# Attention scores as 32-row products in four quarters of the array instead of 64-row products in two halves

## The chip, the cores and the metric

The kernel runs on one core of one Trainium2 chip. The metric is the device time of one execution in microseconds (us). It is given as the median of three runs. A profile comes from one further execution that a hardware profiler recorded. The engines are called by the names of that profile: PE is TensorE (PEld its weight loads), ACT is ScalarE, DVE is VectorE, POOL is GpSimd, SP is SyncE, whose queue issues most DMAs. PSUM is the accumulator memory that PE writes, 8 banks of 128 partitions by 512 fp32 values.

## The reference

The model is a chain of four layers on an image of 48 channels and 128x128 pixels. The change is in the first, a single-head attention over all N = 16384 pixels.

```python
qkv = jnp.einsum('bchw,oc->bohw', x, qkv_w)              # 48 -> 144 channels
qkv = conv3x3_depthwise(qkv, dw_w)
q, k, v = ...                                            # each (b, 16384, 48)
q, k = _l2norm(q), _l2norm(k)
attn = softmax(jnp.einsum('bnc,bmc->bnm', q, k) * temperature, axis=-1)
out = jnp.einsum('bnm,bmc->bnc', attn, v)
return jnp.einsum('bchw,oc->bohw', out, proj_w)
```

The later layers (sweeps of 1-D convolutions, a patch layer and a state-space scan) are not touched.

## The kernel before

**First stage (`attention`, L156).** The image is normalised and convolved on PE, eight image rows (1024 pixels) at a time (`conv`, `take`). `take` leaves the normalised queries and keys of these pixels in fp32. `split` (L410) rounds each to a high part of reduced fp32 ("fp32r") on ACT and takes the remaining low part on POOL. Queries go to a DRAM tensor `qm`, from which `moving(c)` (L196) later fetches chunk `c` of 512 queries. Keys stay in on-chip memory as `kh` (high) and `kl` (low); `join` (L211) copies the first 32 rows of both into further tiles, which the products read as `x`. Early in this stage, between the arrival of the image and the group statistics, `forms` (L120) issues 52 products of zeros on PE: full products of 128 rows, and sets of four products of 32 rows or two of 64 rows, each in its own part of the array.

**Attention proper (`attend`, L481).** There are 32 chunks of 512 queries and 128 tiles of 128 keys. The array is split into two halves of 64 rows. Partitions 0 to 63 hold the first half of the pixels as keys and partitions 64 to 127 the second, so that the two halves of the array compute two key tiles at the same time. A score tile (128 keys by 512 queries) needs 48 channels times three combinations of parts (high with high, high with low, low with high), which are packed into three products of 64 rows: these are `s<-m,kh`, `s<-m,kl` and `s<-m,x` in the profile. Each score tile takes one PSUM bank, from a pool of seven (`ps_s`, L497); the eighth bank is `acc` (`ps_a`).

Six pairs of tiles make a group (`G = 6`, L492), so a chunk has ten groups of twelve tiles and one of eight. `group` (L517) issues a group's scores on PE and the exponentials on ACT (`e<-s,temp`). In the first two pairs of a group DVE copies the second tile out of its bank whole (`e<-s` on DVE), and ACT takes its exponential later from the copy (`e<-e,temp`), in a group of six pairs. `sums` (L539) adds `e` times the values `v` into `acc`: these are full-fp32 products of 128 rows and 64 columns, two at a time in the two halves of the columns, and each is two instructions in the trace (`acc<-e,v`). PE runs the scores of one group, then the sums of the group before it, then the scores of the next.

The order on PE, ACT and DVE is as written: the wrapper `InOrder` (L39) chains each engine's instructions in the order of the calls. Once per chunk `Finish` copies `acc` out (`both<-acc`, on ACT), divides by the softmax's denominator on DVE and writes the result. Another function, `attend_shifted`, is for large temperatures; it is compiled too, but a branch on the temperature skips it here.

Of the kernel before, what the change touches and what calls it, by code (L numbers as in the profile page):

```python
# [19 lines left out]
F32 = mybir.dt.float32  # L20
# [7 lines left out]
C = 48  # L28
H = W = 128
N = H * W  # L30
# [89 lines left out]
def forms(pe, psum, pool):  # L120


    zero = pool.tile([128, CH], F32R, name="rn")
    pe.tc.nc.gpsimd.memset(zero.bitcast(F32), 0.0)
    out = [psum.tile([128, CH], F32, name="p") for _ in range(4)]

    def one(o, at, to, n):
        w, x = zero[at, n : n + to.stop - to.start], zero[at]
        pe.matmul(o[to], lhsT=w, rhs=x, start=True, stop=True)

    def pieces(size):
        return [slice(i, i + size) for i in range(0, 128, size)]

    def full(n):
        for i in range(n):
            one(out[i % 4], slice(0, 128), slice(0, 128), 0)

    def quads(n):
        for _ in range(n):
            for o, at in zip(out, pieces(32)):  # L140
                one(o, at, slice(0, 128), 0)

    full(4)
    quads(5)
    full(4)
    quads(1)
    full(4)
    quads(1)
    full(4)
    for _ in range(4):  # L150
        for o, at in zip(out, pieces(64)):
            one(o, at, slice(0, 128), 0)


@with_exitstack
def attention(ctx, tc, x1, mp, const, ins):  # L156
# [20 lines left out]
    qm = dram.tile([64 + C, N], F32, name="qm")  # L177
    kv = ctx.enter_context(tc.tile_pool(name="l0_kv", bufs=1))

    kh, kl = (kv.tile([128, HALF], F32R, name=n) for n in ("kh", "kl"))  # L180
    rest_k = []

# [12 lines left out]

    def moving(c):  # L196

        m = mp.tile([128, 2, CH], F32R, name="m")
        high, low = qm[0:C, c * CH : (c + 1) * CH], qm[C:, c * CH : (c + 1) * CH]
        for half in range(2):  # L200
            at = 64 * half
            for i, to, x in (
                (0, 0, high),
                (0, C, low[C:]),
                (1, 0, low[0:32]),
                (1, 32, low[0:32]),
            ):
                nc.sync.dma_start(m[at + to : at + to + x.shape[0], i].bitcast(F32), x)
        return m

    def join(cols):  # L211

        i = cols.start // PART
        if len(rest_k) == i:
            rest_k.append(images.tile([128, PART], F32R, name=f"x{i}"))
        to = slice(cols.start - i * PART, cols.stop - i * PART)
        for half in range(2):
            at = 64 * half
            for n, t in enumerate((kh, kl)):
                nc.sync.dma_start(  # L220
                    rest_k[i][at + 32 * n : at + 32 * n + 32, to].bitcast(F32),
                    t[at : at + 32, cols].bitcast(F32),
                )
# [5 lines left out]
    with ExitStack() as a:  # L229
# [3 lines left out]
        fp = a.enter_context(tc.tile_pool(name="l0_f", bufs=4))  # L233
        once = a.enter_context(tc.tile_pool(name="l0_a1", bufs=1))
# [15 lines left out]
        wt = wp.tile([128, 4, 256], F32, name="wt")  # L250
        nc.vector.tensor_mul(wt[:, :, 64:], raw[1], raw[0])
        nc.vector.tensor_copy(wt[:, :, 0:64], wt[:, :, 128:192])
# [14 lines left out]
        values = wt[:, :, 192:256]  # L267
# [11 lines left out]
        forms(pe, ps, rnp)  # L279
# [53 lines left out]
        def conv(p, pv, te, y, first):  # L333

            t, e = te
            both = slice(64, 192) if first >= HALF else slice(0, 128)
# [23 lines left out]
            for dx in range(3):  # L360
                for n in range(2):
                    pe.matmul(
                        rows(half[n]),
                        lhsT=wt[:, dx, 192:256],
                        rhs=t[:, y + 4 * n : y + 4 * n + 4, dx : dx + W],
                        start=(dx == 0),
                        stop=False,
                    )
            for n in range(2):
                rest(half[n], n, slice(192, 256))  # L370

        def take(t0, p, pv):
# [23 lines left out]
            kb = 64 * (t0 // HALF)  # L396
            tk = t0 % HALF
            tv = slice(t0 // 128, t0 // 128 + 8)

            qb = 64 - kb  # L400
# [9 lines left out]
            def split(act, get):  # L410

                for n in range(2):
                    f, hl = own[n], get("hl", n)
                    fq, fk = f[qb : qb + 64], f[kb : kb + 64]
                    hq, lq = hl[qb : qb + 64], hl[kb : kb + 64]
                    at = slice(tk + n * CH, tk + (n + 1) * CH)
                    to = slice(t0 + n * CH, t0 + (n + 1) * CH)
                    act.copy(hq.bitcast(F32R), fq)
                    act.copy(kh[kb : kb + 64, at], fk)
                    nc.gpsimd.tensor_sub(lq.bitcast(F32R), fq, hq)  # L420
                    nc.gpsimd.tensor_sub(
                        kl[kb : kb + 64, at], fk, kh[kb : kb + 64, at].bitcast(F32)
                    )
                    nc.sync.dma_start(qm[0:C, to], hq[0:C])
                    nc.sync.dma_start(qm[C : 64 + C, to], lq)
                if kb:
                    join(slice(tk, tk + 2 * CH))

            def get(name, n):
                return fp.tile([128, CH], F32, name=name)  # L430
# [9 lines left out]
        for b in range(NB):  # L440
# [3 lines left out]
            for y in range(0, R, 8):  # L444
# [3 lines left out]
                conv(p, pv, cur, y, t0)  # L448
# [10 lines left out]
    keys = kh, kl, rest_k  # L459
    with tc.If(small <= bits) as near:  # L460
        attend(tc, keys, v, moving, first, x1, temp, const, ins, last[0:2])
# [19 lines left out]
def attend(ctx, tc, keys, v, moving, m, x1, temp, const, ins, last):  # L481
# [9 lines left out]
    KT = N // 2 // 128  # L491
    G = 6  # L492

    ep = ctx.enter_context(tc.tile_pool(name="l0_e", bufs=G + 4))
# [4 lines left out]


    sides = [slice(0, 64), slice(64, 128)]

    def scores(m, j):
        s = [ps_s.tile([128, CH], F32, name="s") for _ in sides]
        for n in range(3):
            k, at = key_tile(keys, n, j)
            for half, part in enumerate(sides):
                pe.matmul(
                    s[half],
                    lhsT=k[part, at],  # L510
                    rhs=m[part, n // 2],
                    start=(n == 0),
                    stop=(n == 2),
                )
        return s, ep.tile([128, 2, CH], F32, name="e")

    def group(m, js, help):  # L517

        waiting, es = [], []

        def exp(e, half, s):
            act.activation(e[:, half], s, AF.Exp, scale=temp)

        for n, j in enumerate(js):
            s, e = scores(m, j)
            if help and len(js) > 4 and n < 2:
                exp(e, 0, s[0])
                dve.tensor_copy(e[:, 1], s[1])
                waiting.append(e)
            else:  # L530
                exp(e, 0, s[0])
                while waiting:
                    t = waiting.pop(0)
                    exp(t, 1, t[:, 1])
                exp(e, 1, s[1])
            es.append((j, e))
        return es

    def sums(acc, j, e):  # L539

        for half, to in enumerate(sides):
            pe.matmul(
                acc[to],
                lhsT=v[:, half * KT + j, :],
                rhs=e[:, half, :],
                start=(j == 0),
                stop=(j == KT - 1),
            )
# [5 lines left out]
    class Finish:  # L554


        def __init__(self, c, acc):
# [5 lines left out]
            act.copy(self.both, acc)  # L563
# [35 lines left out]
    names = {("f", 0): "xres", ("f", 1): "both", ("hl", 0): "second", ("hl", 1): "y"}  # L599
    own = {key: spare(name) for key, name in names.items()}  # L600

    def get(name, n):
        return own[name, n]
# [4 lines left out]
    behind, finish, acc, ahead = [], None, None, m  # L608
    for c in range(NQ):
        m = ahead  # L610
        for g in range(-(-KT // G)):
            es = group(m, range(g * G, min((g + 1) * G, KT)), c > 0 or g > 1)
            if c and g == 1:
                finish.divide()
            if c and g == 2:
                finish.result()
            if g == 0 and c + 1 < NQ:
                ahead = moving(c + 1)
            if c == 0 and g == 2:
                split(act, get)  # L620
            for i, e in behind:
                if i == 0:
                    acc = ps_a.tile([128, CH], F32, name="acc")
                sums(acc, i, e)
# [3 lines left out]
    for i, e in behind:  # L628
        sums(acc, i, e)
    end()  # L630


def key_tile(keys, n, j):

    if n < 2:
        return keys[n], slice(j * 128, (j + 1) * 128)
    per = keys[2][0].shape[1] // 128
    return keys[2][j // per], slice(j % per * 128, (j % per + 1) * 128)
# [3 lines left out]
def attend_shifted(ctx, tc, keys, v, moving, m, x1, absT, sgn, const, ins, last):  # L642
# [5 lines left out]
    KC = HALF // CH  # L648
# [10 lines left out]
    own = {name: ep.tile([128, 2, CH], F32, name="e") for name in ("f", "hl")}  # L659

    def get(name, n):
        return own[name][:, n]
# [4 lines left out]
    k16 = k16p.tile([128, HALF], F16, name="k16")  # L667
    for i in range(0, HALF, 2048):
# [1368 lines left out]
```

## Time and profile before

| what | us |
|---|---|
| median of three runs (lowest, highest) | 7174.86 (7173.81, 7175.15) |
| profiled execution, its own time | 7166.1 |
| its span, first to last instruction | 7164.0 |
| first stage, up to the first scores | 0 to 244 |
| attention proper | 253 to 3551 |
| later layers | 3551 to 7164 |

The page of the profile lists for each group of instructions its engine, the tiles it writes and reads, shapes, count, busy time and the mean duration of one. A timeline lists single instructions in order of time, with neighbours of the same kind merged: start, length of the merged stretch, count, and in brackets how long the engine had been idle and who ended that. Durations of pipelined instructions overlap, on PE and on ACT, so the distance from start to start is the rate and the duration is the latency.

### The profile page before, as it was taken

What the parts mean: (1) busy time and instruction counts of PE and PEld (TensorE: products, weight loads), DVE (VectorE), ACT (ScalarE), POOL (GpSimd) and SP (SyncE); (2) the same over time, 40 slices, a digit from 0 to 9 for tenths busy, and PEclk for the clock granted to TensorE, in tenths of its full rate; (3) what the DMA queues carried; (4) which work ended last, traced back from release to release, by engine and by line L of the source; (5) the groups of instructions that cost most, each with busy time, mean ns of one, the idle gap of its engine ahead of it and who ended that gap; (6) DMA issues with size and microseconds to landing.
All of it is one profiled execution on the core that took longest, in us unless ns stands there. A gap on an engine that the chain in (4) does not pass through costs nothing.

```text
span 7164.0 us, 200017 instructions
## 1 busy us (share of the span) xinstructions
PE 5826.9 (81%) x89756; PEld 3507.7 (49%) x89756; DVE 3844.0 (54%) x3616; ACT 4601.6 (64%) x6795; POOL 2866.4 (40%) x656
## 2 busy tenths in 40 slices
PE   9999999999999999999999998455555545554555
PEld 3455555555555555555577754343434434344444
DVE  6322212221221122112244544899999999999998
ACT  3677777777777777777741033666666666666665
POOL 3200000000000000000100322899999999999998
PEclk9999999999999999999999999677676766776667
DMA  4200000000000000000010010566566665666775
GB/s 90 54 7 10 10 8 7 10 9 7 10 10 9 7 10 10 9 7 10 17 30 12 16 46 19 156 166 161 160 159 162 162 160 154 165 165 167 179 178 149
DMA packets 201829, 515.82 MB, mean 72 GB/s; under 512 B 41859, under 2 KB 73650, under 8 KB 199058
## 3 DMA queue, kind: packets, MB, share of 16 engines
q1 hardware_dynamic: 189335, 493.23, 26.6%
q8 instruction: 705, 11.55, 0.7%
q10 hardware_dynamic: 11627, 9.71, 0.6%
q14 instruction: 162, 1.33, 0.1%
HBM read 447.73 MB, written 29.36 MB: 67 GB/s over the span
## 4 chain that ended last, share of the span: by engine, by line
PE 60%; DVE 25%; issue 6%; POOL 4%; ACT 2%; DMA 2%; SPq 0%; ACTq 0%; DVEq 0%; POOLq 0%
PE acc L49 25%; DVE h L1789 23%; PE s L49 21%; PE p L49 7%; POOL h L49 3%; PE y L49 2%; PE pp L49 1%; PE pv L49 1%; PE pc L49 1%; DMA du<-rep 1%; DVE xb L49 1%; ACT dA L49 1%; PE po L49 1%; DVE y L49 0%; ACT L49 0%
## 5 line engine op out<-in xcount | busy, mean ns | idle before, releaser
L49 ACT ACTIVATE e<-s,temp 128x512 f32<-128x512 f32 x3460 | 2141.6, 698 | 775.9 <-PE s L49 769.6
L49 POOL TENSOR_TENSOR h<-du,bt 128x3072 f32<-128x3072 f32 (+1 forms) x386 | 2560.1, 6670 | 97.1 <-DMA du<-rep 53.2
L1789 DVE TENSOR_TENSOR_SCAN h<-dA,carry,h 128x1024 f32<-128x1024 f32 x864 | 1939.5, 2324 | 31.6 <-ACT dA L49 26.8
L49 DVE COPY e<-s 128x512 f32<-128x512 f32 x636 | 440.0, 692 | 2626.9 <-PE s L49 2611.9
L49 ACT ACTIVATE dA<-dt,a 128x1024 f32<-128x1024 f32 x1152 | 1287.3, 1118 | 855.7 <-DVE h L1789 845.7
L49 PE MATMUL acc<-e,v 128*64 128x512 f32 x8192 | 1835.2, 596 | 0.0
L49 PE MATMUL y<-h,cw 128*32 128x48 f32 x49152 | 893.1, 245 | 928.6 <-issue 489.7
L49 PEld LDWEIGHTS y<-h,cw 128*32 128x32 f32 x49152 | 804.2, 139 | 1049.6 <-issue 646.8
L854 POOL MEMSET xb<- 128x256 f32 (+1 forms) x2 | 0.8, 410 | 3271.7 <-ACT absT L465 3271.7
L49 PEld LDWEIGHTS acc<-e,v 128*64 128x64 f32 x8192 | 557.0, 137 | 1093.0 <-issue 1090.2
L49 PE MATMUL s<-m,kh 64*128 64x512 f32 x4096 | 848.6, 409 | 8.1 <-ACT e L49 6.5
L49 PE MATMUL s<-m,kl 64*128 64x512 f32 x4096 | 811.8, 391 | 0.0
L49 PE MATMUL s<-m,x 64*128 64x512 f32 x4096 | 801.6, 387 | 0.0
L1789 DVE TENSOR_TENSOR_SCAN h<-dA,h 128x1024 f32<-128x1024 f32 x288 | 635.4, 2271 | 37.3 <-ACT dA L49 29.0
L49 PEld LDWEIGHTS s<-m,kh 64*128 64x128 f32 x4096 | 386.1, 184 | 371.2 <-issue 259.5
L49 PEld LDWEIGHTS s<-m,x 64*128 64x128 f32 x4096 | 387.8, 185 | 89.1
L49 ACT ACTIVATE e<-e,temp 128x512 f32<-128x512 f32 x636 | 420.7, 711 | 0.0
L49 PEld LDWEIGHTS s<-m,kl 64*128 64x128 f32 x4096 | 386.2, 184 | 69.1
L49 PE MATMUL yz<-ev,sel 128*8 128x48 f32 x4096 | 192.6, 260 | 270.6 <-ACT ev L49 268.2
L49 PEld LDWEIGHTS yz<-ev,sel 128*8 128x8 f32 x4096 | 162.2, 106 | 330.3 <-ACT ev L49 302.6
L49 PE MATMUL p<-xb,l_w 112*48 112x78 f32 (+8 forms) x6096 | 226.7, 223 | 17.6 <-DVE xb L49 6.9
L49 PE MATMUL p<-xa,l_w 112*48 112x78 f32 (+8 forms) x6096 | 228.6, 224 | 14.7 <-DVE xa L49 5.9
(223 smaller groups left out, 3915.7 us busy)
## 6 DMA issues: line engine op xcount, KB each, us to landing
du<-rep SPq DMA_DIRECT2D x768, 256.0 KB
dt<-rep SPq DMA_DIRECT2D x768, 256.0 KB
m<-qm SPq DMA_DIRECT2D x128, 64.0 KB
m<-qm SPq DMA_DIRECT2D x64, 96.0 KB
rep<-dd SPq DMA_DIRECT2D x24, 192.0 KB
yd<-ys ACTq DMA_DIRECT2D x256, 12.0 KB
qm<-hl SPq DMA_DIRECT2D x30, 128.0 KB
rest<-xa SPq DMA_DIRECT2D x90, 38.0 KB
```

The source lines that it names most:

```text
L49: ins = method(*args, **kwargs).ins
L854: nc.gpsimd.memset(b[:, lines, pad], 0.0)
L1789: nc.vector.tensor_tensor_scan(h[:, p, k, :], dA, h[:, p, k, :], carry[:, i, k : k + 1] if ci else 0.0, ALU.mult, ALU.add,)
```

## The change

Keys are laid out in one tensor `keys` of 128 partitions by 3 parts by 4096 pixels, a quarter of the pixels in each 32 partitions. Part 0 holds the high parts of channels 0 to 31, part 1 their low parts, and part 2 the high and the low parts of channels 32 to 47, 16 rows each. The queries of a chunk are laid out alike in `mq`, four times. A score tile is now five products of 32 rows (`PASSES`), and the array's four quarters of rows work on four key tiles at once. `turn(n)` issues round `n`: one product in each quarter. The quarters are out of step (`LEAD`), so that their tiles end in different rounds.

A group is eight tiles, in ten rounds, and a chunk has sixteen groups. Of the first three tiles to end in a group, DVE copies the last 224 of the 512 columns to the tile of exponentials, ACT takes the exponential of the first 288 straight from the bank, and after the group's other tiles one ACT instruction takes the exponential of the three copied pieces in place. `acc` is copied out by DVE (`Finish.take`), after the third tile of group 1. The exponentials' tiles are the four `x` tiles that held the image. `split` makes one rounding and one difference over 128 partitions where it made two over 64, and sends keys and queries on by DMA. `join` and `forms` are gone.

```diff
-def forms(pe, psum, pool):
...
-    kh, kl = (kv.tile([128, HALF], F32R, name=n) for n in ("kh", "kl"))
+    keys = kv.tile([128, 3, N // 4], F32R, name="keys")
...
+    mq = [kv.tile([128, 4, CH], F32R, name=f"mq{n}") for n in range(2)]
     def moving(c):
-        m = mp.tile([128, 2, CH], F32R, name="m")
...
+        m = mq[c % 2]
+        src = parts_of[:, :, c * CH : (c + 1) * CH]
+        for r in range(0, 128, 32):
+            nc.sync.dma_start(m[r : r + 32, 0:2].bitcast(F32), src[0:32])
+            for at in (r, r + 16):
+                nc.sync.dma_start(m[at : at + 16, 2:4].bitcast(F32), src[32:C])
         return m
-    def join(cols):
...
-        forms(pe, ps, rnp)
...
             def split(act, get):
...
-                    act.copy(hq.bitcast(F32R), fq)
-                    act.copy(kh[kb : kb + 64, at], fk)
-                    nc.gpsimd.tensor_sub(lq.bitcast(F32R), fq, hq)
...
+                    act.copy(hl[:, 0].bitcast(F32R), f)
+                    nc.gpsimd.tensor_sub(hl[:, 1].bitcast(F32R), f, hl[:, 0])
+                    nc.sync.dma_start(parts_of[:, :, to], hl[0:C])
+                    nc.sync.dma_start(keys[r : r + 32, 0:2, kc].bitcast(F32), hl[64:96])
+                    for i in range(2):
+                        nc.sync.dma_start(
+                            keys[r + 16 * i : r + 16 * i + 16, 2, kc].bitcast(F32),
+                            hl[96 : 64 + C, i],
+                        )
...
 def attend(...):
-    G = 6
-    ep = ctx.enter_context(tc.tile_pool(name="l0_e", bufs=G + 4))
+    R = 4
+    KT = N // 128 // R
+    PASSES = ((0, 0), (0, 1), (1, 0), (2, 2), (2, 3))
+    NP = len(PASSES)
+    LEAD = (0, 0, 1, 3)
+    G = 8
+    ROUNDS = G * NP // R
+    SHARED = 3
+    OWN = 288
...
     ps_s = ctx.enter_context(tc.tile_pool(name="l0_ps", bufs=7, space=PSUM))
     ps_a = ctx.enter_context(tc.tile_pool(name="l0_pa", bufs=1, space=PSUM))
...
+    def turn(n):
+        done = []
+        for r, lead in enumerate(LEAD):
+            at, i = divmod(n + lead, NP)
+            c, j = divmod(at, KT)
+            if n + lead < 0 or c == NQ:
+                continue
+            if i == 0:
+                banks[r] = ps_s.tile([128, CH], F32, name="s")
+            part, x = PASSES[i]
+            rows_ = slice(32 * r, 32 * r + 32)
+            pe.matmul(
+                banks[r],
+                lhsT=keys[rows_, part, j * 128 : (j + 1) * 128],
+                rhs=queries[c][rows_, x],
+                start=(i == 0),
+                stop=(i == NP - 1),
+            )
+            if i == NP - 1:
+                done.append((r * KT + j, banks[r]))
+        return done
...
+        for n in range(ROUNDS):
+            for j, s in turn((c * KT * NP) + g * ROUNDS + n):
...
+                if help and len(es) < SHARED:
+                    dve.tensor_copy(e[:, OWN:], s[:, OWN:])
+                    exp(e[:, :OWN], s[:, :OWN])
+                else:
+                    exp(e, s)
+                es.append((j, e))
+                if then and len(es) == SHARED:
+                    then()
+        if help:
+            late = first[:, 0:SHARED, OWN:]
+            exp(late, late)
...
-            act.copy(self.both, acc)
+            self.acc = acc
+
+        def take(self):
+            dve.tensor_copy(self.both, self.acc)
```

## Prediction

> **What bounds the kernel now.** First the busy times by stretch, to see which engine fills the attention; then the chain that ended last, for the period of a group; then single instructions in the timeline, for rates and latencies.
>
> ```profile
> 253.00:3551.00 3298.00, 3296.79 (x20461) 1682.31 (x20461) 645.14 (x826) 2516.01 (x4132) 5.13 (x4) 1.00 0.03 9
> ```
>
> The columns after the length are PE, PEld, DVE, ACT, POOL, the granted clock and DMA. PE fills the stretch at clock 1.00, ACT 76% of it. The chain between 900 and 1100 us is PE alone:
>
> ```profile
> 954.19 4.35 PE s L49 x36
> 958.54 5.30 PE acc L49 x24
> 963.84 2.99 PE s L49 x24
> ```
>
> A group is 4.35 + 5.30 = 9.65 us. The last group of a chunk has 24 score products (2.99), and its sums, 16 instructions, take 1.72 less than 24 (four steps of 0.43, below). A chunk is 11 x 9.65 - 1.36 - 1.72 = 103.07, 32 chunks 3298: the whole stretch.
>
> One group in the timeline:
>
> ```profile
> 1008.88 0.50 PE L49 MATMUL s<-m,kh 64*128 64x512 f32 x2
> 1009.22 0.40 PE L49 MATMUL s<-m,kl 64*128 64x512 f32 x2
> 1009.46 0.40 PE L49 MATMUL s<-m,x 64*128 64x512 f32 x2
> ...
> 1009.95 2.08 ACT L49 ACTIVATE e<-s,temp 128x512 f32<-128x512 f32 x3 [2.30 <-PE s L49]
> 1010.00 1.39 DVE L49 COPY e<-s 128x512 f32<-128x512 f32 x2 [8.26 <-PE s L49]
> ...
> 1012.91 0.39 PE L49 MATMUL s<-m,x 64*128 64x512 f32 x2
> 1013.15 4.15 ACT L49 ACTIVATE e<-s,temp 128x512 f32<-128x512 f32 x7
> ...
> 1013.23 5.37 PE L49 MATMUL acc<-e,v 128*64 128x512 f32 x24
> 1013.71 0.14 PEld L49 LDWEIGHTS acc<-e,v 128*64 128x64 f32 x2 [0.29 <-issue]
> ```
>
> Two half-array products go together as one round. The first step after a switch of form is 0.34 (1008.88 to 1009.22), the others 0.23. From the last scores to the first sums it is 0.32; sums step by 0.48, then 0.43 (the next weight loads start at 1014.14 and 1014.57). Of the 5.30, 0.48 + 10 x 0.43 leaves 0.52 for the switch back. A bank's last product starts at 1009.46, ACT on it at 1009.95, DVE at 1010.00: 0.49 and 0.54 until a reader starts. Seven exponentials fit in 4.15 though the page gives each 0.698: they start 0.57 apart.
>
> **Rounds of four quarters.** The change's form stands in this trace, in `forms`; the timeline of the weight loads alone, each of which goes just ahead of its product:
>
> ```profile
> 26.79 1.00 PEld L49 LDWEIGHTS p<-rn 32*128 32x128 f32 x20 [0.37 <-issue]
> 28.16 0.76 PEld L49 LDWEIGHTS p<-rn 128*128 128x128 f32 x4 [0.37 <-issue]
> 29.28 0.19 PEld L49 LDWEIGHTS p<-rn 32*128 32x128 f32 x4 [0.36 <-issue]
> 29.71 0.30 PEld L49 LDWEIGHTS p<-rn 128*128 128x128 f32 x2 [0.24 <-issue]
> ```
>
> Five rounds of four take 28.16 - 26.79 = 1.37 us, one round 0.43, switches included. A further round is (1.37 - 0.43) / 4 = 0.235, as for two halves: four products cost what two did. A group of eight tiles then has 10 rounds, the last starting at 0.34 + 8 x 0.235 = 2.22; 0.32 to the sums; 8 steps of sums and the way back, 0.48 + 6 x 0.43 + 0.52 = 3.58. That is 6.12 us, times 512 groups 3133: 165 less than 3298. Ten rounds for eight tiles in place of twelve save more than 160 more groups, with their switches, cost.
>
> The Trainium skill (TensorE: Matmul & The Clock Gate, Measured speedup vs the span model) measured four row tiles of 32 rows by 512 columns at 3.07 times one, not 4. By that a round would be 4 / 3.07 x 0.235 = 0.306, an estimate, and 5120 rounds 364 us dearer. The rows above, taken on this core, decide.
>
> **The banks.** This is the step that decides. The order of the changed program, with its waits, shows what a released bank does. Seven banks go round in the order in which tiles are begun. Counting rounds from 0: quarters 0 and 1 begin tiles in rounds 0 and 5 and end them in 4 and 9, quarter 2 begins in 4 and 9, quarter 3 in 2 and 7. Eight begin per group, and each takes the bank of the tile seven before. So quarter 1's tile in round 5 takes the bank of quarter 3's that was begun in round 7 of the group before and gets its last product in round 1 of this group. Between lie four rounds, 0.94 us. PE's instruction waits for ACT's first exponential of the group, and that for DVE's copy of the same tile: the two engines drain a bank one after the other.
>
> From the first score's start: round 1 starts at 0.34. DVE starts 0.54 later, at 0.88. Its copy of 224 columns: the page has 0.692 for 512; other DVE rows give 1.04 ns per column (0.240 for 78, 0.692 for 512), so 0.39, end 1.27. ACT follows DVE by 0.03 (in the scan, a DVE record ends at 5005.273 and ACT starts at 5005.307): 1.30. Exponential of 288 columns: 0.69 for 512 less 224 x 0.83 ns (1.118 us for 1024 against 0.698), so 0.50, end 1.80. Release to PE, from the first group of chunk 0, where PE waits for ACT:
>
> ```profile
> 258.18 0.76 ACT L49 ACTIVATE e<-s,temp 128x512 f32<-128x512 f32 x1
> ...
> 258.99 0.18 PEld L49 LDWEIGHTS s<-m,kh 64*128 64x128 f32 x1 [0.39 <-ACT e L49]
> 258.99 0.50 PE L49 MATMUL s<-m,kl 64*128 64x512 f32 x1
> 259.32 0.39 PE L49 MATMUL s<-m,kl 64*128 64x512 f32 x1
> ```
>
> 0.05 from the end of the exponential (258.94) to PE: 1.85. Round 5 was due at 0.34 + 4 x 0.235 = 1.28, so PE stands 0.57. After such a wait the next round comes 0.34 later (258.99 to 259.32), not 0.235, since the weights were not loaded ahead: 0.10 more. Behind the waiting product stand quarters 2 and 3 in the same round and all that follows, the sums too. A group becomes 6.12 + 0.67 = 6.79, and 512 make 3476, 178 more than 3298. Even is at (3298 - 3133) / 512 = 0.32 per group.
>
> Other releases, with round 5 at 1.85, round 7 at 2.43 and round 9 at 2.90: the second shared tile (ended in round 3, 0.81) is copied from 1.35, exponential from 1.77, free at 2.32 for round 7; the third (round 4) free at 2.71 for round 9. Margins 0.1 and 0.2 are less than a round, by which weights are loaded ahead, so each may cost up to 0.1. ACT: five exponentials at 0.57, three of 288 columns at 0.57 - 0.19 = 0.38, and one of 672 from on-chip memory, (1.32 - 0.71) + 0.13 = 0.74: 4.74 per group, below 6.12. It ends its late piece at about 6.2, and its next exponential is due at 6.79 + 1.30.
>
> Bounds of the stall. Below: copy 0.35; exponential 0.41 (the page's ACT copy of 288 columns); no cost of refilling. Free at 0.88 + 0.35 + 0.03 + 0.41 + 0.05 = 1.72, stall 0.44: 3358, +60. Above: both margins missed, 0.2 more: 3579, +281. I take 0.67, all of whose terms come from the nearest rows.
>
> **The rest.** `forms` gone: the statistics' aggregate ends at 30.06 and its product on PE starts at 33.54 behind `forms`, so 3.4 us gained; PE idles longer there and its clock, 0.50 from 38 to 48 us already, may take that back (0 to -3.4; I take -3). `split` on ACT and POOL halves, but PE is busy 100% between 100 and 200 us, which hides it. In its last call two POOL differences (1.26 each) go, but eight DMAs on SP's queue remain at 0.5 each, so ACT's first exponential at 252.46 stays, +-2 us. `both<-acc` on DVE (0.69) follows the third copy, about 2.1 to 2.8, before the sums at 3.2; the divide behind it on DVE (0.42 + 0.68 + 3.34) ends at 7.3, before the next group's first copy at 6.79 + 0.88 = 7.67. The queries' DMAs are issued fifteen groups ahead of their use. `attend_shifted` is not run.
>
> Sum: +178 - 3 = +175, on the profiled 7166.1: 7341. The median stands 8.8 above that execution, so I forecast 7174.86 + 175 = 7350.
>
> **Rivals.**
> 1. The drain is quicker than PE's need (faster). If both engines read one bank at once, it is free at 0.34 + 0.49 + 0.50 + 0.05 = 1.38: stall 0.10 + 0.10, 512 x 6.32 = 3236, -62, time about 7110 (with no stall at all -165 and 7007). It decides once the bank is free by 1.28 + 0.32 - 0.10 = 1.50 instead of 1.85. Against it: the changed program has ACT wait for DVE, and the bounds above stay over 0.32. For it: all four quarters need not stand still in hardware as they do in my sum. 0.11, and 0.02 for a tie.
> 2. The clock falls (slower). PE would wait once in each group, 0.6 of 6.8 us. Before, with PE waiting 0.39 for each exponential, the windows show 0.50 in 252 to 256 us, after an idle stretch, 0.93 in 256 to 260 and 1.00 in 262 to 272: short waits did not bring it down. Halving it for 5% of the stretch costs 174 more: 7524. It leaves my range once 3% of the stretch runs at half (106 of 3476). 0.05.
> 3. The four quarters don't run together while ACT and DVE read other banks, the change not doing what it says: at two by two, 5120 x 0.235 = 1203 more. No sign of it in `forms`, where nothing was read meanwhile. 0.02.
>
> The skill (same page, A second HAM failure mode: psum-queue depth-cycling) describes rival 2, short idle times at PSUM that make the clock swing. In the row above they did not; by the rule the time would be rival 2's.
>
> **How the numbers follow.** My forecast has 0.80, between 7174.86 + 60 - 3 = 7232 and 7174.86 + 281 = 7456. To leave no more than two in ten out I reach down to 7195, a stall of 0.37, toward rival 1. Slower by over 0.2% (14 us, about what can be told from no change) 0.87, within 0.02, faster 0.11.
>
> **What would show it.** PE idle before `s`, some 0.6 us once per group, ended by ACT's exponential of 288 columns; group period 6.79; rounds 0.235 apart; DVE's 224 columns 0.39 and the 288 columns 0.50 long; clock 1.00. It is wrong if the 288-column exponential starts before DVE's copy of that tile ends, if round 5 follows round 4 without a gap, or if the period is under 6.44.

## The result and the profile after

The changed kernel takes 7347.64 us (median of four runs, 7346.34 to 7354.23). The kernel before took 7175.0 us in the runs beside it, and the ratio of the runs is 1.0243, 95% interval 1.0225 to 1.0261: slower by 2.4%. The forecast was 7350.

The profiled execution took 7346.34 us, with a span of 7344.5. The attention, from the first score product to the last sum, is 3482.7 us long where it was 3305.6, so 177.1 us of the 180.5 by which the span grew lie there. The same stretch that carried the reading of before, with the columns as there (PE, PEld, DVE, ACT, POOL, granted clock, DMA):

```profile
253.00:3730.00 3477.00, 3383.12 (x28620) 1561.48 (x28616) 769.29 (x1751) 2521.03 (x4602) 2.52 (x2) 1.00 0.05 14
```

The clock is 1.00 as before, and no engine but PE is near its limit. PE is no longer busy throughout. The chain that ended last was PE alone; now it runs through three engines in this and other groups:

```profile
913.51 0.40 DVE x L49
913.91 0.02 issue
913.93 0.51 ACT x L49
914.45 0.04 issue
914.49 1.43 PE s L49 x17
915.92 3.58 PE acc L49 x16
```

DVE copies 224 columns out of a bank, 0.02 later ACT takes the exponential of the other 288, and 0.04 to 0.05 after that PE can start a product into this bank. The four pieces ahead of PE's product are 0.98 us long. The timeline of one group, PE's weight loads and the queues left out, shows where PE stood meanwhile:

```profile
1000.93 1.66 PE L49 MATMUL s<-mq,keys 32*128 32x512 f32 x21
1001.80 1.07 DVE L49 COPY x<-s 128x224 f32<-128x224 f32 x3 [5.71 <-issue]
1002.23 4.18 ACT L49 ACTIVATE x<-s,temp 128x288 f32<-128x288 f32 x8 [1.86 <-DVE x L49]
...
1002.78 1.43 PE L49 MATMUL s<-mq,keys 32*128 32x512 f32 x19 [0.19 <-ACT x L49]
...
1004.15 3.65 PE L49 MATMUL acc<-x,v 128*64 128x512 f32 x16
```

ACT's merged line is three exponentials of 288 columns and five of 512. The first 21 of a group's 40 score products go without a break: five rounds of four, and quarter 0 of round 5. The 22nd is the tile of quarter 1 that waits for its bank. It starts 1.85 after the group began (1000.93 to 1002.78), after DVE at 0.87 and ACT at 1.30. In the medians over the 354 groups between 1000 and 3400 us quarter 0 starts round 5 at 1.27 and quarter 1 at 1.846, a gap of 0.575. The next group starts at 1007.73, and the median period is 6.790.

The page's table must be read with care here:

```profile
L49 DVE COPY x<-s 128x224 f32<-128x224 f32 x1530 | 547.8, 388 | 2692.2 <-issue 2184.7
L49 PE MATMUL s<-mq,keys 32*128 32x512 f32 x20480 | 1589.0, 412 | 95.8 <-ACT x L49 94.5
```

It puts PE's idle time for ACT at 94.5 us, 0.19 for each of 511 waits, a third of the gap. A product's record lasts about 0.4 us while the next starts 0.23 later, so the records of the products before the wait reach into it. What a wait costs is read from start to start.

### The profile page after: what moved, and what is told of

The parts are those of the page before. It is cut to its first block, busy times and chain, and to the rows that moved or that the text cites. A ratio compares the mean times of both kernels' runs of the same rounds, so it can differ in the third digit from the quotient of the medians.

```text
span 7344.5 us, 215883 instructions
## 1 busy us (share of the span) xinstructions
PE 5902.6 (80%) x97896; PEld 3381.2 (46%) x97896; DVE 3968.3 (54%) x4540; ACT 4589.7 (62%) x7242; POOL 2825.8 (38%) x623
## 4 chain that ended last, share of the span: by engine, by line
ACT 29%; DVE 27%; PE 24%; issue 14%; POOL 4%; DMA 2%; SPq 1%; ACTq 0%; DVEq 0%; POOLq 0%
ACT x L49 27%; DVE h L1767 21%; PE p L49 7%; PE acc L49 6%; PE s L49 4%; DVE x L49 3%; POOL h L49 3%; PE y L49 2%; PE pp L49 1%; DMA du<-rep 1%; DVE xb L49 1%; PE pc L49 1%; ACT dA L49 1%; PE pv L49 1%; PE po L49 1%
## 5 line engine op out<-in xcount | busy, mean ns | idle before, releaser
L49 ACT ACTIVATE x<-s,temp 128x512 f32<-128x512 f32 (+1 forms) x4096 | 2145.1, 630 | 951.7 <-DVE x L49 951.7
L49 DVE COPY x<-s 128x224 f32<-128x224 f32 x1530 | 547.8, 388 | 2692.2 <-issue 2184.7
L49 PE MATMUL acc<-x,v 128*64 128x512 f32 x8192 | 1871.0, 599 | 0.0
L49 PE MATMUL s<-mq,keys 32*128 32x512 f32 x20480 | 1589.0, 412 | 95.8 <-ACT x L49 94.5
L49 PEld LDWEIGHTS s<-mq,keys 32*128 32x128 f32 x20480 | 1023.0, 183 | 853.7 <-ACT x L49 730.0
L49 PEld LDWEIGHTS acc<-x,v 128*64 128x64 f32 x8192 | 542.6, 136 | 1064.7 <-issue 1053.2
L49 ACT ACTIVATE x<-x,temp 128x672 f32<-128x672 f32 x510 | 457.6, 897 | 0.0
L49 PEld LDWEIGHTS p<-xb,l_w 112*48 112x48 f32 x6096 | 193.3, 123 | 51.6 <-DVE xb L49 36.3
L49 PEld LDWEIGHTS p<-xa,l_w 112*48 112x48 f32 x6096 | 192.6, 122 | 49.6 <-DVE xa L49 30.8
L49 PE MATMUL pc<-wt,xa 128*128 128x288 f32 x768 | 198.2, 415 | 0.0
```

Of the source, the lines that this page charges most:

```text
L49: ins = method(*args, **kwargs).ins
```

## Experiments

In the first four runs the kernel before took 7166.58 us beside them, in the last four 7167.94. Ratios are to these. The expectations start from 7347, which stood beside a kernel before of 7175.0, so some 8 us of each difference in time are the runs' and not the edit's.

**ACT drains every bank alone** (`e1_act_alone`):

```diff
-                if help and len(es) < SHARED:
-                    dve.tensor_copy(e[:, OWN:], s[:, OWN:])
-                    exp(e[:, :OWN], s[:, :OWN])
-                else:
-                    exp(e, s)
+                exp(e, s)
```
(and without the late exponential)

> ACT drains all eight tiles of a group alone; the copies by DVE and the late exponential are gone. Theory (PE waits in round 5 for the bank of the first tile drained, free at 0.34 + 0.54 + 0.39 + 0.03 + 0.50 + 0.05 = 1.85 us after the group's first score): by ACT alone the bank is free at 0.34 + 0.49 + 0.69 + 0.05 = 1.57, so the first wait shrinks by 0.28, but the third bank, behind two exponentials of 512 columns, now comes 0.1 too late for round 9 and costs 0.2 with the refill. Period 6.80 - 0.28 + 0.2 = 6.72, time about 7347 - 40 = 7307. Rival A (ACT's work sets the period, as its share of the chain suggests): its work per group falls from about 4.95 to 8 x 0.57 = 4.56, time about 7347 - 0.39 x 512 = 7147. Rival B (two engines drain faster than one): slower than 7347.

It took 7331.97 us, ratio 1.0231 (1.0214 to 1.0248), with a period of 6.769, where 7307 and 6.72 were expected. The ratio alone doesn't tell it from the changed kernel, whose interval overlaps; the trace does. ACT's work as the bound (7147) is excluded. Round 5 goes on at 1.600 instead of 1.846:

```profile
1000.41 1.23 PEld L49 LDWEIGHTS s<-mq,keys 32*128 32x128 f32 x21 [0.81 <-issue]
...
1001.29 4.73 ACT L49 ACTIVATE x<-s,temp 128x512 f32<-128x512 f32 x8 [2.06 <-PE s L49]
...
1002.03 0.99 PEld L49 LDWEIGHTS s<-mq,keys 32*128 32x128 f32 x17 [0.39 <-ACT x L49]
1003.19 0.18 PEld L49 LDWEIGHTS s<-mq,keys 32*128 32x128 f32 x2 [0.16 <-ACT x L49]
```

So the help of DVE, put in front of ACT's exponential of the same bank, makes the first bank come free 0.25 us later than ACT alone would. The period falls by 0.02 only, because the third bank now comes late. In the medians over some 440 groups ACT's second exponential ends at 2.13, so with the 0.05 of the release the second bank is free at 2.18, just when quarter 3 starts its tile in round 7 (2.18). That tile is not late, but its next product follows 0.34 later instead of 0.23. The third exponential ends at 2.71; its bank is free at 2.76 and holds up quarter 2 in round 9 (2.756 instead of 2.64; the last line above).

**The third tile copied whole by DVE, the first two by ACT alone** (`e2_third_by_dve`):

```diff
-                if help and len(es) < SHARED:
-                    dve.tensor_copy(e[:, OWN:], s[:, OWN:])
-                    exp(e[:, :OWN], s[:, :OWN])
+                if help and len(es) == SHARED - 1:
+                    dve.tensor_copy(e, s)
```
(and the late exponential over the third tile alone)

> The first two tiles of a group are drained by ACT alone; the third is copied whole by DVE and its exponential taken last. Theory: first bank free at 1.57 (wait 0.29 + 0.10), second at 1.41 + 0.69 + 0.05 = 2.15 for round 7, due at 2.15, third at 1.04 + 0.54 + 0.69 + 0.05 = 2.32 for round 9, due at 2.6: one wait of 0.39 in place of 0.67. Period 6.80 - 0.28 = 6.52, time about 7347 - 143 = 7204. Rival A (ACT's work): 8 x 0.57 + 0.04 = 4.60 per group, time about 7165, the same as with ACT alone within 20 us. Rival B (drained by two engines is faster): slower than 7347.

7271.65 us, ratio 1.0148 (1.0131 to 1.0165), period 6.641 where 7204 and 6.52 were expected. The wait for the third bank is gone and the first is as in the run above (1.59). The missing 0.11 is the second bank, free at 2.17 (the exponential ends at 2.12) and taken at that moment: the next product of that quarter comes at 2.51 instead of 2.40. Two engines on different banks are here better than two on one bank, but one drain of 1.23 us still does not fit into four rounds.

**All quarters in step** (`e3_in_step`):

```diff
-    LEAD = (0, 0, 1, 3)
+    LEAD = (0, 0, 0, 0)
```

> LEAD = (0, 0, 0, 0): the four quarters begin and end their tiles in the same rounds; the work of each engine is unchanged. Theory: in round 5 the fourth tile needs the bank of the first one ended in round 4, started at 1.04, free at 1.04 + 0.54 + 0.39 + 0.03 + 0.50 + 0.05 = 2.55, where round 5 is due at 1.28: wait 1.27 + 0.10 in place of 0.67. Period 6.80 + 0.70 = 7.50, time about 7347 + 358 = 7705. Rival A (ACT's work) and any theory in which rounds or switches of form cost more: no work changes, 7347 within 20 us.

7683.27 us, ratio 1.0725 (1.0707 to 1.0743), period 7.438, against 7705 and 7.50:

```profile
1004.82 1.67 PE L49 MATMUL s<-mq,keys 32*128 32x512 f32 x23
...
1007.32 1.43 PE L49 MATMUL s<-mq,keys 32*128 32x512 f32 x17 [0.83 <-ACT x L49]
```

All four tiles now end in round 4, and quarter 3's tile of round 5 stands until 2.498 after the group's start (2.55 expected). The offset of the quarters is worth 0.65 us per group. The loss follows the time from a tile's last product to the product that takes its bank, as the theory says.

**A short drain of the first three banks** (`e4_short_drain`). The first three tiles are read over 8 columns only, and three full exponentials from the fourth tile's bank take the place of theirs. ACT's work is not less than in the first run (eight full exponentials and three short ones); the three banks are free almost at once. The result is not the attention's any more; the run serves the timing alone.

```diff
-                if help and len(es) < SHARED:
-                    dve.tensor_copy(e[:, OWN:], s[:, OWN:])
-                    exp(e[:, :OWN], s[:, :OWN])
+                if len(es) < SHARED:
+                    exp(e[:, :8], s[:, :8])
...
+                if len(es) == SHARED + 1:
+                    for i in range(SHARED):
+                        exp(es[i][1], s)
```
(and without the late exponential)

> The first three tiles of a group are read by ACT over 8 columns only, so that their banks come free early; their exponentials are then taken from the fourth tile's bank, so three of eight tiles have another tile's exponentials. ACT still takes eight exponentials of 512 columns per group, PE does the same products, DVE drains nothing. Theory: the first bank is free at 0.34 + 0.49 + 0.27 + 0.05 = 1.15, before round 5 at 1.28: no wait, period 6.10 to 6.15, time 7347 - 0.70 x 512 = 6990 to 7015, also 160 below the kernel with two halves. Rival A (ACT's work, 8 x 0.57 + 3 x 0.15 = 5.0 per group, not less than now): 7347 or more. Rival C (rounds of four quarters, or switches of form, cost more beside the drains than in the zero products of the trace before): a fall of less than half of that, 7180 to 7347.

7007.16 us, ratio 0.9779 (0.9762 to 0.9795), period 6.122:

```profile
1001.28 2.61 PE L49 MATMUL s<-mq,keys 32*128 32x512 f32 x40
1002.07 0.27 ACT L49 ACTIVATE x<-s,temp 128x8 f32<-128x8 f32 x1 [0.55 <-PE s L49]
1002.53 5.11 ACT L49 ACTIVATE x<-s,temp 128x8 f32<-128x8 f32 x10 [0.19 <-PE s L49]
1003.81 3.65 PE L49 MATMUL acc<-x,v 128*64 128x512 f32 x16
```

All 40 products of a group go in one run, rounds 0.23 apart, and the attention takes 3141.7 us, 163.9 less than before. That is the gain of the rounds by themselves. With the changed kernel's period it makes the stall 6.790 - 6.122 = 0.668 us. It also excludes ACT as the bound: here it works more, 2744 of 3137 us (87%) against 2521 of 3477, and PE is busy 3134.5 of the 3137.

**Groups of four tiles** (`e5_groups_of_four`). If the loss is a bank that is wanted back too early, sums between its last product and its next tile should remove it, at the price of twice as many switches between scores and sums.

```diff
-    LEAD = (0, 0, 1, 3)
-    G = 8
+    LEAD = (0, 0, 0, 0)
+    G = 4
```
(and ACT alone, as in the first run)

> The changed kernel with groups of four tiles in place of eight: all quarters in step, five rounds to a group, every bank drained by ScalarE alone. A tile then takes the bank of the tile seven before it, which is the first tile of the group before or a tile of the group before that: free 1.2 us after the fifth round starts, while PE is in its sums (1.9 us). Theory (the drain of one bank against four rounds is the loss): no wait ended by ScalarE before a score product, a period of 1.04 + 0.32 + 0.48 + 2 x 0.43 + 0.52 = 3.22 us for four tiles (6.43 for eight, where the changed kernel has 6.79), 1024 x 3.22 = 3297 in place of 512 x 6.79 = 3476, so about 180 us under the changed kernel, within 0.3% of the kernel before on either side. Rival (ScalarE's own rate or something else about products of 32 rows beside a drain is what costs): PE still stands in front of scores and the period for four tiles is near 3.4, the time within 60 us of the changed kernel.

7182.63 us (7174.82 to 7191.08), ratio 1.0019 (1.001 to 1.0028). In the timeline PE's lines have no idle time in brackets, and its pieces follow one another without a gap:

```profile
1000.69 1.44 PE L49 MATMUL s<-mq,keys 32*128 32x512 f32 x20
...
1002.05 1.94 PE L49 MATMUL acc<-x,v 128*64 128x512 f32 x8
...
1003.92 1.44 PE L49 MATMUL s<-mq,keys 32*128 32x512 f32 x20
```

The period is 3.237 for four tiles, 6.47 for eight, where the kernel before needs 9.646 x 8 / 12 = 6.43. The expectation had 3.22; the rest is 0.01 each in the way to the sums (0.33) and in the sums with the way back (1.87), which over 1024 groups are 17 us. The attention takes 3317.5 us, 12 more than before: the saved rounds go into the switches.

**The kernel before without `forms`** (`e6_before_no_forms`):

```diff
-        forms(pe, ps, rnp)
```

> The kernel before, without the call of forms. The prediction took 3 us for this part of the change (0 to 3.4); the two traces showed the first convolution 2.1 us earlier. Theory: 1 to 3 us under the kernel before, the first products of the convolution at about 41.7 in place of 43.6 us, the clock at 0.50 from about 30 us on. Rival (the time comes back further on, because the idle stretch takes the clock down): no difference in the start of the attention, 252.5 us.

7162.61 us, ratio 0.9989 (0.998 to 0.9998). The first lines are of the kernel before, the second pair of this run:

```profile
43.56 7.80 PE L49 MATMUL p<-band,wt 128*128 128x512 f32 x12
...
58.34 5.32 PE L49 MATMUL p<-band,wt 128*128 128x512 f32 x12
```

```profile
41.67 7.47 PE L49 MATMUL p<-band,wt 128*128 128x512 f32 x12
...
56.13 5.32 PE L49 MATMUL p<-band,wt 128*128 128x512 f32 x12
```

The convolution starts 1.9 us earlier and is 2.2 us ahead in its second round. The first exponential of the attention keeps that lead (250.25 against 252.46). The product after the statistics' aggregate starts 3.07 us earlier (30.47 against 33.54). In between the products of `p<-band,ident` take 7.16 us instead of 6.33, and the granted clock from 30 to 50 us is 0.60 instead of 0.74: part of the gain goes to the clock. The medians differ by 5.3 us, more than the 2.2 that the traces show; the interval holds both.

**Four `hl` buffers in the first stage** (`e7_four_hl`). In the first stage the changed kernel's trace has a wait of PE that no step of the prediction names:

```profile
ACT hl L49 <- DMA keys<-hl: 21.9, 10, 7.6
```

```profile
179.04 3.68 PE L49 MATMUL pss<-sq,blk 128*128 128x512 f32 x4 [2.09 <-ACT sq L49]
```

The first is from the list of waits (us in total, times, longest), the second from the timeline. The rounding into `hl` has to wait until the DMAs have emptied the buffer, and on ACT the squares `sq` for the norms stand behind it. PE waits 2.09 us for them, and the four products then take 3.68 us. The run gives every second call of `split` two more buffers:

```diff
+                if name == "hl" and (t0 // (2 * CH)) % 2:
+                    return mq[1][:, 2 * n : 2 * n + 2].bitcast(F32)
```

> The changed kernel, in which split writes into four hl buffers in turn in place of two (the other two lie in the second buffer of the queries, which is free in that stage). Theory (the wait of ScalarE's cast for the DMA that empties hl holds up the squares queued behind it, PE stands 2.1 us at 177 us and the clock falls to 0.50 for 3.4 us): ScalarE's waits for that DMA, 21.9 us in 10, are gone or nearly so, PE is busy without a break from 100 to 200 us with the clock at 1.00, and the attention starts about 4 us earlier (245.9 to about 242); the time is 4 us or 0.05% lower, at the edge of what the comparison can tell. Rival (PE's idle time there comes from the DMA queue itself, not from the number of buffers): the same 2 us of PE idle, and the attention starts at 246.

The waits for the DMA are gone and PE does not stand:

```profile
100.00:200.00 100.00, 100.00 (x330) 37.43 (x330) 77.28 (x52) 32.20 (x58) 21.88 (x25) 1.00 0.54 116
```

```profile
177.64 1.98 PE L49 MATMUL pss<-sq,blk 128*128 128x512 f32 x4
```

The first scores, of the changed kernel and then of this run:

```profile
245.89 2.10 PE L49 MATMUL s<-mq,keys 32*128 32x512 f32 x25 [1.26 <-ACT late L49]
```

```profile
242.79 2.10 PE L49 MATMUL s<-mq,keys 32*128 32x512 f32 x25 [1.26 <-ACT late L49]
```

They start 3.1 us earlier. So the number of buffers was the cause of the wait. The size of the gain is less sure: in the five other runs with two buffers the first scores start at 244.1 to 247.4 us, with four, here and in the last run, at 242.8 and 243.3. The time, 7344.92 us, ratio 1.0244 (1.023 to 1.0258), does not show it: from the last sum on, the later layers, the same in all runs, took between 3611 and 3623 us in the profiled executions.

**Groups of four and four `hl` buffers together** (`e8_both`), the edits of the two runs.

> Groups of four tiles and four hl buffers together. Theory: the two savings add, about 184 us under the changed kernel and 4 us under the groups of four alone: 0.9985 to 0.9998 of the kernel before. Rival: the groups of four already show what there is, and nothing is added.

7177.77 us, ratio 1.0011 (1.0002 to 1.002), 4.9 under the groups of four alone; the intervals of the two overlap, so that the savings add is not shown, nor that they don't. It is slower than expected because the period is 3.235 and not 3.22. The only version under the kernel before that keeps the whole computation is that kernel without `forms`.

## Why the prediction was right

**The rounds of four quarters.** Forecast 0.235 us a round, 6.12 a group, 165 us less. Measured without the stall: 0.233, 6.122 and 163.9 less. A round of four takes as long as the round of two did before, also while ACT and DVE read other banks; rival 3 falls. The Trainium skill's page TensorE: Matmul & The Clock Gate, section Measured speedup vs the span model, has a speed-up of 3.07 for four row tiles. By that the prediction estimated a round at 0.306; the short drain's rounds took 0.233, and the measurement decides.

**The banks.** Each link was there: DVE at 0.87 after the group's start (0.88), the copy 0.39 to 0.40 long (0.39), ACT at 1.30 (1.30), its exponential 0.50 (0.50), PE at 1.85 (1.85), the stall 0.575 (0.57), the next round 0.34 later (0.34). The period of 6.79 is the forecast's. The experiments show that it is this chain: a quick drain gives the whole 0.668 back, a drain by one engine gives 0.25 back at this bank, more distance between last product and next tile gives it back too, and less distance makes it longer. The other two margins, 0.1 and 0.2, were left open at up to 0.1 each; they cost nothing in the changed kernel. They were larger than the sum had them, 0.18 and 0.25: DVE's second copy starts at 1.26 and not at 1.35, and the two banks are free at 2.24 and 2.63, for products at 2.42 and 2.88. In the second experiment, where a bank came free at the moment it was wanted, that did cost the 0.11.

**Rivals 1 and 2.** Rival 1 said that two engines might read one bank at once. The program has ACT wait for DVE, and ACT followed DVE 510 times; most of the 951.7 us that ACT stood ahead of that, 1.87 each time, it would have stood for the scores. What two readers at once would do, no run here shows. The rival's other half was that a stall below 0.32 would make the change faster. The short drain, with no stall, is faster. That its 7007.16 is the very time that the rival named is luck: it lies 159 us under the kernel before of its own runs, where the rival had 168. Rival 2: a wait of 0.575 in every 6.79 us left the clock at 1.00 in the 3477 us of the attention. The Trainium skill (TensorE: Matmul & The Clock Gate, A second HAM failure mode: psum-queue depth-cycling) tells of short idle times between products that make the clock swing; these waits did not.

**The small terms** were less good. `forms` gave 2.1 us, not 3: the clock took more back than I allowed. That `split` costs nothing because PE is busy 100% between 100 and 200 us failed. Its cover was gone since the change itself put a new wait ahead of PE's work: PE was busy 97.91 of those 100 us. The lead of 2.1 us that `forms` gave was a lag of 1.7 at the first score (245.89 against 244.17), so 3.9 us were lost between: 2.1 of PE standing, and most of the rest in the four products behind it (3.68 us instead of 1.98), at a lower clock (0.94 from 170 to 200 us). Four buffers gave 3.1 of it back, by one execution of each. I had looked at the two engines whose work was halved, and not at the DMAs that must empty the buffer before ACT may fill it again, nor at what stands behind `split` on ACT. ACT's first exponential came 3.8 us earlier (248.66), outside the 2 us allowed: before, ACT's load of the table ahead of it stood 4.52 us for the DMA `qm<-hl`, and now it does not.

By profiled executions the sum is off by 5: 180.2 us more where 175 were forecast, and the missed 3.9 is most of that. By medians it is off by 2.4 the other way. The step that took the 8.8 us between the median and the profiled execution of before over to after has no ground: after's profiled execution lies 1.3 us under its median. That the forecast of 7350 is only 2.4 off is so in part luck: the 8.8 too much covers the 5 and the 1.3 too little. A difference of some us between two executions is not the kernel's.

## What to carry to other kernels

When products become quicker, work out anew when each PSUM bank is wanted back: from the last product of a tile to the first product of the tile that takes its bank, against the whole drain, with the start of the reader and the release. Where the program has a second engine's help on the same bank come in series, it lengthens that drain, as here; give the help another bank, or put other work of PE between, which costs more switches between forms (groups of four took the stall away and were still 0.2% over the kernel before). A form with fewer rounds is worth what is left after the wait, and a run of the same kernel with the drain cut short tells at once how much that could be.

## What the runs showed of the hardware

A tile that is begun just as its bank comes free starts on time, but the next product of that quarter of the array starts 0.34 us after it, not 0.23. In the second experiment this cost 0.11 us per group at the second bank; in the first it lies behind the wait for the third bank. The traces show what the bank holds up: the weight load of the tile's first product. In the short drain that load starts 0.23 us ahead of its product. In the changed kernel, at the second bank, it starts 0.18 ahead, when the bank comes free, and the product and the next one are on time. In the first two experiments load and product start together.

How long a wait of PE must be to cost clock can be bounded in the first stage. Around 178 us PE stands once for the squares in each run of the changed program with two `hl` buffers: 1.10 us in the short drain, where the granted clock from 170 to 190 us stays at 1.00, and 1.75 to 2.09 us in the five others, where it is 0.91. The waits of 0.575 us in the attention left it at 1.00.
